# An attention and feed-forward kernel: three layout changes moved to DMA transfers, a feed-forward from exact bf16 parts, and one of fourteen additions done by an accumulating transfer

## The chip, the cores and the metric

One core of a Trainium2 chip runs the whole program. The metric is the device time of one execution in microseconds (us). The kernel before took 4421.93 us as the median of three runs (4421.24 to 4422.01).

## What is computed

The input `x` is 4 sequences of 2048 rows of 512 float32 values. Queries, keys and values are projections with three 512x512 matrices, for 16 heads of 32 columns. Attention is added to `x` and each row is normalised. A feed-forward with the signs of a 512x512 matrix follows, and it is scaled and shifted by column and clipped; it is added to the normalised rows, and each row is normalised again:

```python
q = (x @ Wq.T).reshape(N, S, H, hd).transpose(0, 2, 1, 3)   # k, v the same way; H = 16, hd = 32
energy = jnp.einsum('nhqd,nhkd->nhqk', q, k)
attn = jax.nn.softmax(energy / jnp.sqrt(jnp.float32(hd)), axis=3)
out = jnp.einsum('nhql,nhld->nhqd', attn, v)
...
x = _layernorm(x + out)
w = (weights >= 0.0) * 2.0 - 1.0
y = jnp.clip(jnp.einsum('bsi,oi->bso', x, w) * scale + bias, -100.0, 100.0)
x = _layernorm(x + y)
```

Everything is float32, and the kernel keeps float32 products.

## The kernel before

The work is cut into 16 groups `n`: one sequence `b` and four heads (`g`) each. A group has four blocks `qb` of 512 queries, and a block has 16 steps, one for each chunk `kc` of 128 keys. So there are 64 blocks and 1024 steps. The engines are named PE (matrix products), DVE (vector), ACT (activations and copies), POOL (GpSimd) and SP (which issues transfers).

In each step PE does this, in this order:

- `scores` (L306, L312): for four heads, minus the row maximum (three bf16 parts against ones) plus keys times queries. ACT takes the exponentials into a tile `p` of 128x2048 float32 (L319). There are four such tiles in turn (`ppool`).
- `max_unit` (L247): scores of a later block, 22 steps ahead (`LEAD`), for the row maxima. DVE reduces three of the four heads out of PSUM (L254), and ACT copies the fourth to a tile `moved`, which DVE reduces at the end of the step.
- fillers: projections (L206), transposes, feed-forward, sums. A planner gives each a first and a last step and hands out at most two large ones in odd steps.
- `weighted` (L330): every second step, two chunks of probabilities times values into one PSUM bank, which DVE adds to `oT` (L342).

After these, `add_up` lets POOL add the chunk's `p` to `acc` (L350): 14 additions of 128x2048 a block, of which the first takes two chunks. Then come the actions that `at(step, ...)` put at the end of a step: loads, statistics, normalisation, stores. Each engine runs its own instructions in the order in which the program emits them, and PSUM has eight banks, which `take` and `give` hand out by a running estimate of when each comes free.

Three things at the edge of a block matter here. Five steps ahead of a block `max_parts` (L279 to L283) makes the final row maxima and cuts them into three bf16 parts, and `max_rows` turns them with four PE transposes (L290), which ACT copies to `negm` (L295). Some three steps after a block, `denominators` sums the exponentials over keys: PE multiplies the last `p` and `acc` by ones (L356), ACT copies the result to `dT` (L382), and `reciprocals` turns it back with four PE transposes (L390) for DVE (L397). `add_attention` turns `oT` (L390), multiplies by the reciprocals (L414), adds columns of `x` (L418) and stores to a DRAM tensor `res`.

When all four groups of a sequence are done, `Finish` takes blocks of 512 rows, as four tiles of 128 rows: `stats` (L463, L464), `norm` (L489), `turn` (four PE transposes L499, one ACT copy L502 to `nT`), `ffn` in three thirds of 172, 172 and 168 columns (four float32 products each, L510; then DVE adds the bias from PSUM, clips in PSUM and adds to the row, L515, L516, L518), and `stats` and `norm` again. This runs beside the attention of the next sequence, so the first quarter of the time has none of it. The last two of the 16 blocks of rows are finished at the end of the program, in whole width. The signed and scaled weights are made once by POOL (L148, L150) from the raw matrix.

On DVE, every operation with two tensors reads at least one of them from PSUM.

Of the kernel before, what the change touches and what calls it, by code (L numbers as in the profile page):

```python
# [20 lines left out]
def kernel(  # L21
# [35 lines left out]
    stage = ctx.enter_context(tc.tile_pool(name="stage", bufs=4))  # L57
# [9 lines left out]
    work = ctx.enter_context(tc.tile_pool(name="work", bufs=2))  # L67
# [37 lines left out]
    ident_bf = const.tile([P, P], BF16, name="ident_bf")  # L105
    nc.vector.tensor_copy(ident_bf, ident)
# [38 lines left out]
    def sign_weights():  # L145

        ws = raws["ws"]
        nc.gpsimd.tensor_scalar(ws, ws, 0.0, 2.0, ALU.is_ge, ALU.mult)  # L148
        for oc in range(DC):
            nc.gpsimd.tensor_scalar(  # L150
                ws[:, oc, :], ws[:, oc, :], 1.0, scale_t[:, oc : oc + 1], ALU.subtract, ALU.mult
            )

    raws = {n: load_weight(w, n) for n, w in (("wk", wk), ("wq", wq))}
    scale_t = const.tile([P, DC], F32, name="scale_t")
    bias_bc = const.tile([P, D], F32, name="bias_bc")

    def load_rest():
        for n, w in (("wv", wv), ("ws", w_ffn)):
            raws[n] = load_weight(w, n)  # L160
        nc.sync.dma_start(out=scale_t, in_=ffn_scale.rearrange("(c p) -> p c", p=P))
        nc.sync.dma_start(out=bias_bc, in_=ffn_bias.partition_broadcast(P))
# [15 lines left out]
    rec = {}  # L178

# [95 lines left out]
    def max_parts(n, qb, i):  # L275
# [7 lines left out]
        nc.vector.tensor_tensor(sp[:, :, :, 2], nm, sp[:, :, :, 1], ALU.subtract)  # L283

    def max_rows(n, qb):
        sp = split[qb % 2]
        i = take()
        pt = ps[:, i, : QB // 2].bitcast(BF16)
        for qc in range(NTQ):
            nc.tensor.transpose(  # L290
                pt[:, ts(qc, P)], sp[:, qc, :, :].rearrange("p h d -> p (h d)"), ident_bf
            )
        negm[n, qb] = small.tile([P, QB], BF16, tag="negm", name="negm")
        runs("full", 0.23)
        nc.scalar.copy(negm[n, qb], pt)  # L295
        give(i, "ACT", 0.6)
# [48 lines left out]
    def add_up(n, qb, kc, p, before):  # L345
        if kc == 1:
            acc[n, qb] = apool.tile([P, HG, QB], F32, tag="acc", name="acc")
        if 0 < kc < (NT // 2 if is_last(n, qb) else NT - 1):
            a = acc[n, qb]
            nc.gpsimd.tensor_tensor(a, before if kc == 1 else a, p, ALU.add)  # L350
        if kc == NT - 1:
            last_p[n, qb] = p
# [20 lines left out]
    def denominators(n, qb):  # L373
# [3 lines left out]
        else:  # L377
            b = take()
            ones_times(b, last_p.pop((n, qb)), True, False)
            ones_times(b, acc.pop((n, qb)), False, True)  # L380
        dT = once.tile([P, QB], F32, tag="dT", name="dT")
        nc.scalar.copy(dT, ps[:, b, :])  # L382
        give(b, "ACT", 0.6)
        acc[n, qb] = dT

# [7 lines left out]

    def reciprocals(n, qb):
        i, pd = turn_back(acc.pop((n, qb)))
        rec[n, qb] = small.tile([P, NTQ, HG, 1], F32, tag="rec", name="rec")
        nc.vector.reciprocal(rec[n, qb], pd[:, :, :, 0:1])  # L397
        give(i, "DVE", 0.3)
# [30 lines left out]
    class Finish:  # L429
        def __init__(self, b, g):  # L430
            self.b, self.g = b, g
            self.mv, self.rs, self.nb, self.nT, self.rows_rs = {}, {}, {}, {}, {}

# [60 lines left out]

        def turn(self, j):
            i = take()
# [4 lines left out]
            self.nT[j] = work.tile([P, DC, P], F32, tag="nT", name="nT", bufs=4)  # L501
# [3 lines left out]
        def ffn(self, j, third):  # L505
            cols = slice(0, D) if third is None else slice(THIRDS[third], THIRDS[third + 1])
            i = take()
            py = ps[:, i, : cols.stop - cols.start]
            for c in range(DC):
                nc.tensor.matmul(  # L510
                    py, lhsT=self.nT[j][:, c, :], rhs=wT["ws"][:, c, cols],
                    start=(c == 0), stop=(c == DC - 1),
                )
            runs("full", 6.8e-3 * (cols.stop - cols.start))
            nc.vector.tensor_tensor(py, py, bias_bc[:, cols], ALU.add)  # L515
            nc.vector.tensor_scalar(py, py, MAX_VAL, -MAX_VAL, ALU.min, ALU.max)  # L516
            dst = self.row(j)[:, cols]
            nc.vector.tensor_tensor(dst, dst, py, ALU.add)  # L518
            give(i, "DVE", 0.5 + 3.1e-3 * (cols.stop - cols.start))
# [30 lines left out]
    def finish(b, qb, a, every, w, lag):  # L550
        f = Finish(b, qb)
        at(a, f.load)
        for j in range(NTQ):
            at(a + 2 + j, f.stats, 1, j)
        at(a + 6, f.rstd, 1)
        at(a + 7 + lag, f.shift, 1)
        for j in range(NTQ):
            t = a + 8 + lag + every * j
            at(t, f.norm, 1, j)
            turned = task("small", t + 1, t + 3, f.turn, j)  # L560
            for k in range(3):
                task("big", t + 2, t + w, f.ffn, j, k, after=turned)
            at(t + w, f.stats, 2, j)
        e = a + 9 + lag + every * (NTQ - 1) + w
        at(e, f.rstd, 2)
        at(e + 1 + lag, f.shift, 2)
        for j in range(NTQ):
            at(e + 2 + lag + j, f.norm, 2, j)
        at(e + 5 + lag, f.store)

    def finish_last(qb, last):
# [4 lines left out]
        late = qb == NQB - 2  # L576
        for j in range(NTQ):
# [3 lines left out]
        ffns = []  # L581
        for j in range(NTQ):
            t = a + 5 + (j if late else 2 * j)
            by = t + 6
            at(t, f.norm, 1, j)
            if late:
                by = total + (-1, 1, 4, 5)[j]
            turned = task("small", t + 1, t + 3, f.turn, j, after=ffns[j - 2] if j > 1 else None)
            for k in [None] if late else range(3):
                ffn = task("big", by if late else t + 2, by, f.ffn, j, k, after=turned)  # L590
            ffns.append(ffn)
# [222 lines left out]
```

## Time and profile before

| | before |
|---|---|
| median of three runs | 4421.93 us |
| the profiled execution | 4420.69 us |
| its span in the profile | 4418.7 us |
| granted clock of PE | 0.999 |
| busy PE | 4380.8 us (99%) |
| busy POOL | 4083.3 us (92%) |
| busy DVE | 3320.2 us (75%) |
| busy ACT | 3048.4 us (69%) |

The span runs from the first to the last instruction of one execution. The busy time of an engine is the time in which at least one of its instructions is under way; for PE the ends of matrix products are modelled, so that starts are the safer thing to compare. A row of the groups view has line, engine, operation, output and inputs with their shapes, how many there are, then the busy time, the mean duration of one in ns, and the idle time before them with what ended it. A float32 product shows as two records.

### The profile page before, as it was taken

The page shows a single profiled execution, that of the slowest core. Times are in us where ns is not written, and L with a number is a line of the kernel's source. Part 1 is how long each engine was busy: PE and PEld are TensorE (multiplying, and loading weights), DVE is VectorE, ACT ScalarE, POOL GpSimd, SP SyncE. Part 2 cuts the span into 40 slices and gives each one's busy share as a digit, 9 for nine tenths or more (in the row PEclk, how much of TensorE's full clock was granted, in tenths as well). Part 3 has the DMA queues.
Part 4 walks back from the last instruction along what each step waited for, and adds up shares of the span by engine and source line. Part 5 has one row for each costly group of instructions (what it writes and reads, how often), then busy time and mean ns, then how long its engine had stood idle before and what let it go on. Part 6 is the DMA issues. An engine that isn't in the chain of part 4 may idle for free.

```text
span 4418.7 us, 94451 instructions
## 1 busy us (share of the span) xinstructions
PE 4380.8 (99%) x38648; PEld 2261.4 (51%) x38648; DVE 3320.2 (75%) x5909; ACT 3048.4 (69%) x6493; POOL 4083.3 (92%) x940
## 2 busy tenths in 40 slices
PE   9999999999999999999999999999999999999998
PEld 5554444454555555555555555555555555555443
DVE  6777777777777777777777777777777777777774
ACT  5666666676667667677676766767667676767675
POOL 3999999999999999999999999999999999999994
PEclk9999999999999999999999999999999999999999
DMA  3000000010000000011000000001000000000001
GB/s 91 6 11 11 6 11 11 9 39 28 6 11 30 6 20 20 6 42 32 20 20 6 30 11 16 20 7 48 16 20 20 18 18 20 16 20 30 13 23 45
DMA packets 98019, 92.30 MB, mean 21 GB/s; under 512 B 4272, under 2 KB 73904, under 8 KB 97584
## 3 DMA queue, kind: packets, MB, share of 16 engines
q1 hardware_dynamic: 92304, 82.07, 6.2%
q8 instruction: 302, 4.95, 0.5%
q10 hardware_dynamic: 5280, 4.19, 0.3%
q14 instruction: 133, 1.09, 0.1%
HBM read 53.74 MB, written 32.51 MB: 20 GB/s over the span
## 4 chain that ended last, share of the span: by engine, by line
PE 89%; POOL 8%; ACT 1%; issue 1%; DVE 1%; DMA 0%; ACTq 0%; POOLq 0%; DVEq 0%
PE ps L330 19%; PE ps L247 18%; PE ps L312 18%; PE ps L206 15%; POOL acc L350 8%; PE ps L306 7%; PE ps L510 5%; PE ps L356 3%; PE ps L390 2%; PE ps L499 1%; PE ps L195 1%; ACT p L319 1%; DVE part L254 1%; PE ps L290 0%; ACT xg_last L489 0%
## 5 line engine op out<-in xcount | busy, mean ns | idle before, releaser
L350 POOL TENSOR_TENSOR acc<-acc,p 128x2048 f32<-128x2048 f32 x825 | 3743.2, 4537 | 106.1 <-ACT p L319 49.3
L319 ACT ACTIVATE p<-ps 128x512 f32<-128x512 f32 x4096 | 2115.0, 604 | 1148.4 <-PE ps L312 1113.8
L254 DVE TENSOR_REDUCE part<-ps 128x1 f32<-128x512 f32 x3072 | 1934.8, 684 | 821.1 <-PE ps L247 820.2
L247 PE MATMUL ps<-kT,qT 32*128 32x512 f32 x8192 | 1098.1, 590 | 0.0
L312 PE MATMUL ps<-qT,kT 32*128 32x512 f32 x8192 | 1070.7, 590 | 0.0
L330 PE MATMUL ps<-p,vv 128*32 128x512 f32 x8192 | 983.6, 598 | 0.5 <-ACT p L319 0.3
L247 PEld LDWEIGHTS ps<-kT,qT 32*128 32x128 f32 x8192 | 524.0, 185 | 379.8 <-issue 221.0
L254 DVE TENSOR_REDUCE part<-moved 128x1 f32<-128x512 f32 x1024 | 691.2, 675 | 1.7 <-ACT moved L266 1.6
L266 ACT COPY moved<-ps 128x512 f32<-128x512 f32 x1024 | 634.5, 620 | 21.8 <-PE ps L247 16.7
L330 PEld LDWEIGHTS ps<-p,vv 128*32 128x32 f32 x8192 | 220.3, 109 | 685.6 <-issue 346.5
L306 PE MATMUL ps<-negm,ones_bf 32*128 32x512 bf16 x4096 | 434.9, 384 | 3.9 <-ACT p L319 1.3
L312 PEld LDWEIGHTS ps<-qT,kT 32*128 32x128 f32 x8192 | 405.6, 184 | 38.3 <-issue 20.4
L350 POOL TENSOR_TENSOR acc<-p 128x2048 f32<-128x2048 f32 x64 | 290.8, 4544 | 132.4 <-ACT p L319 132.3
L342 DVE TENSOR_TENSOR oT<-ps,oT 128x512 f32<-128x512 f32 x448 | 309.8, 692 | 90.1 <-PE ps L330 57.6
L306 PEld LDWEIGHTS <-ones_bf 32*128 32x128 bf16 x4096 | 104.3, 91 | 496.9 <-issue 438.3
L206 PEld LDWEIGHTS ps<-wvT,xT 128*128 128x128 f32 x2048 | 244.6, 191 | 67.7 <-ACT p L319 62.1
L206 PE MATMUL ps<-wvT,xT 128*128 128x128 f32 x2048 | 270.3, 280 | 1.4 <-ACT p L319 0.5
L206 PEld LDWEIGHTS ps<-xT,wkT 128*128 128x128 f32 x2048 | 242.4, 191 | 48.2 <-ACT p L319 46.7
L206 PE MATMUL ps<-xT,wkT 128*128 128x128 f32 x2048 | 265.1, 279 | 0.5 <-ACT p L319 0.2
L206 PE MATMUL ps<-xT,wqT 128*128 128x128 f32 x2048 | 262.2, 277 | 1.1 <-ACT p L319 1.0
L510 PE MATMUL ps<-wsT,nT 128*128 128x172 f32 (+2 forms) x1408 | 259.3, 329 | 2.4 <-ACT nT L502 1.1
L206 PEld LDWEIGHTS ps<-xT,wqT 128*128 128x128 f32 x2048 | 245.2, 192 | 25.5 <-ACT p L319 23.0
(74 smaller groups left out, 1831.2 us busy)
## 6 DMA issues: line engine op xcount, KB each, us to landing
xs<-in_L_attn_x_dram SPq DMA_DIRECT2D x64, 256.0 KB, 2.8
xc<-in_L_attn_x_dram SPq DMA_DIRECT2D x60, 256.0 KB, 3.2
res<-xc SPq DMA_DIRECT2D x60, 256.0 KB, 2.4
xg<-res SPq DMA_DIRECT2D x12, 1024.0 KB, 6.1
out_dram<-xg SPq DMA_DIRECT2D x12, 1024.0 KB, 4.8
xg_last<-res SPq DMA_DIRECT2D x4, 768.0 KB, 6.1
out_dram<-xg_last SPq DMA_DIRECT2D x3, 1024.0 KB, 4.3
raw_wk<-in_L_attn_Wk_dram ACTq DMA_DIRECT2D x4, 256.0 KB, 6.3
```

The costliest lines, as they stand in the source:

```text
L206: nc.tensor.matmul(pp, lhsT=lhs(c), rhs=rhs(c), start=(c == 0), stop=(c == DC - 1))
L247: nc.tensor.matmul(ps[:, banks[h], :], lhsT=qT[n, qb][rows, ts(qc, P)], rhs=kT[n][rows, ts(kb, QB)], start=True, stop=True,)
L254: nc.vector.tensor_reduce(part[:, qc, h : h + 1, kb], src, AX.X, ALU.max, negate=True)
L266: nc.scalar.copy(moved, ps[:, banks[-1], :])
L306: nc.tensor.matmul(ps[:, banks[h], :], lhsT=ones_bf[rows, :], rhs=negm[n, qb][rows, :], start=True, stop=False,)
L312: nc.tensor.matmul(ps[:, banks[h], :], lhsT=kT[n][rows, ts(kc, P)], rhs=qT[n, qb][rows, :], start=False, stop=True,)
L319: nc.scalar.activation(p[:, h, :], ps[:, banks[h], :], AF.Exp, scale=SM_SCALE)
L330: nc.tensor.matmul(pb[cols, :], lhsT=vv[n][:, kc, cols], rhs=p[:, h, :], start=(i == 0), stop=(i == 1),)
L342: nc.vector.tensor_tensor(outs[n, qb], pb, outs[n, qb], ALU.add)
L350: nc.gpsimd.tensor_tensor(a, before if kc == 1 else a, p, ALU.add)
L356: nc.tensor.matmul(ps[h * HD : (h + 1) * HD, b, :], lhsT=ones, rhs=p[:, h, :], start=start, stop=stop,)
L510: nc.tensor.matmul(py, lhsT=self.nT[j][:, c, :], rhs=wT["ws"][:, c, cols], start=(c == 0), stop=(c == DC - 1),)
```

## The change

- `max_rows` is gone: `max_parts` ends with a transposing DMA transfer, issued by SP, from the 128x512 bf16 parts to `negm`.
- `turn` and the float32 `ffn` are replaced for 14 of the 16 blocks of rows (56 tiles). ACT copies the normalised row to bf16 (`part_high`), DVE subtracts that (`less_high`), ACT copies the rest to bf16 (`part_middle`), DVE subtracts again (`part_low`), one action a step; a transposing transfer turns the 128x1536 bf16 parts to `nT`. `ffn` is then twelve bf16 products a third, with weights of plus and minus one. ACT copies each third to a tile `y` in SBUF. DVE multiplies by the scale (`scaled`), adds the bias and clips (`clipped`), and adds to the row (`added`). Tiles follow each other by 12 steps (10 in the third sequence) instead of 13 and 11.
- For 63 of 64 blocks the sums go by DMA: ACT copies them, SP stores four rows of 512 to DRAM, and SP loads them as 128x16 single values; DVE's reciprocal is put two steps after.
- The addition of the chunk `kc` = 14 is a transfer on POOL's queue that adds `p` to `acc` in SBUF.
- The signs and the scaled weights are made by twelve DVE operations, one every two steps, from step 80 on.
- `stage` has three buffers instead of four, and `work` one instead of two.

```diff
+        negm[n, qb] = small.tile([P, QB], BF16, tag="negm", name="negm")
+        nc.sync.dma_start_transpose(
+            out=negm[n, qb].rearrange("p (t q) -> p t q", t=NTQ),
+            in_=sp.rearrange("p t h d -> p (t h d)"),
+        )
...
-        if 0 < kc < (NT // 2 if is_last(n, qb) else NT - 1):
+        if 0 < kc < (NT // 2 if is_last(n, qb) else NT - 2):
             a = acc[n, qb]
             nc.gpsimd.tensor_tensor(a, before if kc == 1 else a, p, ALU.add)
+        elif kc == NT - 2 and not is_last(n, qb):
+            nc.gpsimd.dma_start(out=acc[n, qb], in_=p, accum_op=ALU.add)
...
+    def columns_of_sums(n, qb):
+
+        dT = acc.pop((n, qb))
+        rows = dram.tile([HG, QB], F32, tag="sums", name="sums", bufs=2)
+        nc.sync.dma_start(out=rows, in_=dT.rearrange("(h r) q -> h r q", h=HG)[:, 0, :])
+        sums_of[n, qb] = small.tile([P, HG * NTQ], F32, tag="sums", name="sums")
+        with nc.allow_non_contiguous_dma(reason="2048 single sums"):
+            nc.sync.dma_start(
+                out=sums_of[n, qb], in_=rows.rearrange("h (t p) -> p (h t)", p=P)
+            )
...
+        def part_high(self, j):
+            self.parts[j] = work.tile([P, 3, D], BF16, tag="parts", name="parts")
+            nc.scalar.copy(self.parts[j][:, 0, :], self.row(j))
...
+        def less_high(self, j):
+            self.left[j] = work.tile([P, D], F32, tag="left", name="left")
+            nc.vector.tensor_tensor(
+                self.left[j], self.row(j), self.parts[j][:, 0, :], ALU.subtract
+            )
...
+        def part_middle(self, j):
+            nc.scalar.copy(self.parts[j][:, 1, :], self.left[j])
...
+        def part_low(self, j):
+            parts = self.parts.pop(j)
+            nc.vector.tensor_tensor(
+                parts[:, 2, :], self.left.pop(j), parts[:, 1, :], ALU.subtract
+            )
...
+            nc.sync.dma_start_transpose(
+                out=self.nT[j], in_=parts.rearrange("p k d -> p (k d)")
+            )
...
+        def ffn(self, j, third):
+
+            cols = slice(THIRDS[third], THIRDS[third + 1])
+            i, py = self.times_weights(j, ws_bf, cols, 0.86)
...
+            nc.scalar.copy(self.y[j][:, cols], py)
+            give(i, "ACT", 0.3)
+
+        def scaled(self, j):
+            nc.vector.tensor_tensor(self.y[j], self.y[j], scale_bc, ALU.mult)
+
+        def clipped(self, j):
+            nc.vector.tensor_tensor(self.y[j], self.y[j], bias_bc, ALU.add)
+            nc.vector.tensor_scalar(self.y[j], self.y[j], MAX_VAL, -MAX_VAL, ALU.min, ALU.max)
+
+        def added(self, j):
+            nc.vector.tensor_tensor(self.row(j), self.row(j), self.y.pop(j), ALU.add)
...
+    def parted(f, t, j):
+
+        at(t, f.norm, 1, j)
+        at(t + 2, f.part_high, j)
+        at(t + 3, f.less_high, j)
+        at(t + 4, f.part_middle, j)
+        at(t + 5, f.part_low, j)
...
+            t = a + 13 + every * j
+            parted(f, t, j)
+            by = t + every - 1
             for k in range(3):
-                task("big", t + 2, t + w, f.ffn, j, k, after=turned)
+                task("big", t + 7, by, f.ffn, j, k)
+            at(by, f.scaled, j)
+            at(by + 2, f.clipped, j)
+            at(by + 3, f.added, j)
+            at(by + 4, f.stats, 2, j)
```

## The prediction

> **What bounds the kernel now.** I read the page's busy row first, then its chain, then POOL's timeline block by block, then one step's timeline. The busy row and the groups:
>
> ```profile
> PE 4380.8 (99%) x38648; PEld 2261.4 (51%) x38648; DVE 3320.2 (75%) x5909; ACT 3048.4 (69%) x6493; POOL 4083.3 (92%) x940
> PE ps L330 19%; PE ps L247 18%; PE ps L312 18%; PE ps L206 15%; POOL acc L350 8%; PE ps L306 7%; PE ps L510 5%; PE ps L356 3%; PE ps L390 2%; PE ps L499 1%; PE ps L195 1%; ACT p L319 1%; DVE part L254 1%; PE ps L290 0%; ACT xg_last L489 0%
> ...
> L350 POOL TENSOR_TENSOR acc<-acc,p 128x2048 f32<-128x2048 f32 x825 | 3743.2, 4537 | 106.1 <-ACT p L319 49.3
> L342 DVE TENSOR_TENSOR oT<-ps,oT 128x512 f32<-128x512 f32 x448 | 309.8, 692 | 90.1 <-PE ps L330 57.6
> ```
>
> PE is full, but 8% of the chain is POOL's additions. POOL's timeline tells where:
>
> ```profile
> 418.26 4.57 POOL L350 TENSOR_TENSOR acc<-p 128x2048 f32<-128x2048 f32 x1
> 422.90 59.90 POOL L350 TENSOR_TENSOR acc<-acc,p 128x2048 f32<-128x2048 f32 x13
> 482.76 4.56 POOL L350 TENSOR_TENSOR acc<-p 128x2048 f32<-128x2048 f32 x1
> ...
> 1463.68 4.54 POOL L350 TENSOR_TENSOR acc<-p 128x2048 f32<-128x2048 f32 x1 [0.64 <-ACT p L319]
> ...
> 1478.35 50.69 POOL L350 TENSOR_TENSOR acc<-acc,p 128x2048 f32<-128x2048 f32 x11 [0.21 <-ACT p L319]
> 1531.21 4.54 POOL L350 TENSOR_TENSOR acc<-p 128x2048 f32<-128x2048 f32 x1 [2.17 <-ACT p L319]
> ```
>
> From 418 to 934 us and once more at 1065 a block takes 64.5 us with no gap: 14 additions at 4.607 us from start to start. POOL bounds these nine blocks. Later, where the feed-forward runs beside attention, a block takes 67.5 us and POOL sits idle for some 4 us of it: PE bounds, but POOL is inside an addition 94% of the time (63.5 of 67.5).
>
> **What goes from PE.** I count from start to start, since ends are modelled.
> - Turning maxima: L290's four transposes start 56 ns apart, and the next float32 product starts 0.256 us after the fourth: 0.42 us x 64 = 27 us.
> - Turning sums: 63 x 4 transposes at 0.109 us = 27 us. Turning rows: 56 x 4 x 0.109 = 24 us.
> - Feed-forward: a float32 third is eight passes 0.146 us apart, 1.17 us. A bf16 third is twelve passes. Their pitch is not in the trace; L290 gives 56 ns for 128 columns, so 75 ns for 172, and L306 (four of 512 columns in 0.216 us) gives 72. That is 0.89 us a third. Where a float32 product follows, the 0.2 us of L290's exit is added; in the new order that is so for some 37 thirds. 168 x 0.28 - 37 x 0.2 = 40 us.
>
> Sum: 118 us, where PE bounds. In the nine POOL-bound blocks the dropped addition counts instead: 64.5 falls to 13 x 4.607 = 59.9 us plus the issue of the transfer, or to what PE needs there (about 60); I take 61.5, so 27 us in place of the 8 us of PE. Net gain about 135 us. ACT loses two copies and gains five per tile; at 69% that stays hidden.
>
> **What comes in on DVE.** Out go 3 x (0.335 + 0.345 + 0.332) = 3.0 us a tile (L515, L516, L518). In come six operations of 512 columns: five at L342's 0.69 us and the clip (0.35 to 0.7), about 4 us. By load alone nothing happens: DVE is at 77% in this stage (207.7 of 269.3 us in the window from 1397.2).
>
> But all six have only SBUF operands, which no DVE operation with two tensors has now. One row of before is near, a DVE cast from SBUF to SBUF at the program's start:
>
> ```profile
> 1.24 0.98 POOL L119 MEMSET split<- 128x512 bf16 x2
> 1.32 0.98 DVE L106 CAST ident_bf<-ident 128x128 bf16<-128x128 f32 x1 [1.32 <-POOL ident masks.py:199]
> ```
>
> 128 elements took 0.98 us, more than the 0.69 us of 512 elements in L342, and the cast ended 0.08 us after POOL's two memsets. The Trainium skill (SBUF — State Buffer, section "Who interferes with whom") states the rule that fits and that speaks against this change: DVE's second pair of SBUF ports is GpSimd's only pair, a DVE operation with two SBUF inputs, or in a two-port mode, contends with a GpSimd operation that reads SBUF, and the later one "fully blocks" until the other ends. The trace shows this beside memsets only, not beside additions. By the rule, such an operation waits out the 4.54 us addition that is under way; by load, it costs 0.69 us and is hidden. I take the rule, since L106 is the only row of its kind.
>
> How much delay can DVE take? Here is a step, with `stats` where the change puts its operations (after the reduction of `moved`):
>
> ```profile
> 1411.47 9.17 POOL L350 TENSOR_TENSOR acc<-acc,p 128x2048 f32<-128x2048 f32 x2
> 1412.49 0.68 DVE L254 TENSOR_REDUCE part<-moved 128x1 f32<-128x512 f32 x1
> 1412.76 1.03 PE L247 MATMUL ps<-kT,qT 32*128 32x512 f32 x8
> 1413.08 0.68 DVE L463 BATCH_NORM_STATS2 st<-xg 128x6 f32<-128x512 f32 x1
> 1413.90 1.85 DVE L254 TENSOR_REDUCE part<-ps 128x1 f32<-128x512 f32 x3
> 1416.09 0.39 PE L306 MATMUL ps<-negm,ones_bf 32*128 32x512 bf16 x4
> ```
>
> A blocked operation here would wait from 1413.1 to 1416.0, run to 1416.7, and only then would the three maxima free their banks. I did this for each of the 744 steps from 1130 to 4350 us. The wait is what is left of POOL's instruction when `moved` is done: 2.18 us on average. The room is the least, over the next DVE instructions, of the time between one's end and PE's next write of its bank, plus DVE's idle time until then: median 1.5 us, a tenth under 0.8, a tenth over 2.6. Wait plus 0.69 us less room, where positive, averages 1.45 us. That is PE standing still, and what queues behind on DVE are the maxima and `oT`, which PE needs.
>
> Per tile there are five steps with such an operation, so 56 x 5 x 1.45 = 406 us. As blocks get longer, POOL is inside an addition less (60 us of 73, not 94%): times 0.85, 345 us. The clip follows the bias addition, and POOL's next addition may come in between: 0 to 4.5 us each; I take a third, 56 x 1.5 x 0.85 = 70 us. POOL's own delay, 6 x 0.7 us a tile, is covered by the addition it lost; without that it would bound the block (64.5 + 4.2 > 67.5).
>
> **Transfers.**
> - nT: issued at the end of step t+5, wanted by PE's fillers in t+7, about 4.7 us after DVE's place in t+5. 384 KB lies between `xs` (256 KB, 2.8 us) and `xg` (1024 KB, 6.1 us), so 3.4 us for a plain transfer; for transposes no row exists, so 3 to 8 us. At 3.4 nothing, at 8 about 4 us x 52 tiles. I take 20 us. Ahead of it on SP stand only transfers whose producers are emitted earlier.
> - negm: 128 KB, five steps (about 19 us) ahead, hidden unless it takes that long.
> - Sums: a store (2.0 us is the nearest, `out_dram<-xg_last`) and a load of 2048 single values (`scale_t`, 512 values, 2.5 us; I take 4), some 7 us with issue. The reciprocal stands two steps later, about 9.5 us after ACT's copy. Hidden, with 2 us to spare; DVE waits if it is later, 63 x the excess, at most 100 us.
> - The accumulating transfer: 1 MB, 4.8 us for a plain store to perhaps 12. It starts after POOL's 13th addition; PE wants the sum, and ACT the `p` tile, four steps after its chunk. Room about 10 us. I take nothing; 63 x 2 us if it takes 12. Its issue on POOL (1 to 3 us) has the lost 4.6 us as cover.
>
> Sum: 345 + 70 + 20 - 135 = +300 us on the profiled 4420.7, which is 1.2 us under the median: 4725.
>
> **Rivals.**
> - DVE does not wait for a whole addition (ports shared, or only memset and cast collide). For it: the DVE rows here all run beside additions at a steady 0.69 us; but they read PSUM. Then 0.69 us goes into room of 1.5 us, and what stays is -135 + 20 to 50 us: 4305, 4285 to 4385. It decides at a wait of 0.8 us; below that the change is faster.
> - A part of the wait (half an addition at most, or five operations where POOL is between blocks): 4390 to 4560.
> - A transfer is late: if the transposes took 15 us, PE would wait 11 us x 52 tiles, +570 us, alone enough for 4860; against it, the landing times above. That transposing transfers work element by element is the form in which the change would not do what it says.
>
> **Numbers.** The full wait 0.64 (4560 to 4940), a part of it 0.13, no wait 0.20, late transfers 0.03. Predicted 4725. The range 4340 to 4900 leaves out the better part of the no-wait case and the top of the full wait. Faster by over 0.2% (9 us, about what a measurement of this kernel can tell from no change): 0.22; within 0.2%: 0.02; slower: 0.76.
>
> **What would show it.** Right: the five new DVE rows with a mean near 2.9 us instead of 0.69, a row of PE waiting for DVE's maxima, POOL's busy share near 80%, blocks of some 73 us in the last three sequences and of about 61.5 us at 420 to 930 us. Wrong: means below 1.2 us in these rows, or a long wait of PE for `nT`, `negm` or `acc`, or of DVE for `sums`.

## The result, and the profile after

The changed kernel takes 4994.95 us (median of four runs, 4990.74 to 5003.59), against 4421.59 us for the kernel before on the same chip: a ratio of 1.1299 (95% interval 1.1280 to 1.1319). It is slower by 573 us where I forecast 300 (4725 us), and lies above the range, which ended at 4900.

The page of the changed kernel, its busy row, the granted clock in 40 slices, the chain by line, and the groups that answer to those shown of before:

```profile
PE 4542.3 (91%) x38588; PEld 2278.8 (46%) x38588; DVE 4019.0 (81%) x5752; ACT 3098.0 (62%) x6653; POOL 3878.8 (78%) x935
...
PEclk9999999999999999999999999999999999999988
...
PE ps L248 12%; PE ps L306 11%; PE ps L324 11%; POOL acc L345 11%; DVE part L255 9%; PE ps L207 7%; PE ps L300 5%; DMA nT<-parts 4%; PE ps L565 3%; DVE parts L535 3%; DVE y L589 3%; DMA acc<-p 2%; PE ps L353 2%; DVE y L585 2%; ACT p L313 2%
...
L345 POOL TENSOR_TENSOR acc<-acc,p 128x2048 f32<-128x2048 f32 x762 | 3496.6, 4589 | 363.8 <-ACT p L313 315.1
```

PE has fewer instructions than before (38,588 for 38,648), yet 161 us more busy time, and is down to 91% of the span. The chain now holds DVE (L255, L535, L589, L585) and two transfers, `nT` and `acc`. POOL, the co-bound of before, is at 78% and idles behind ACT. A busy time that rises while work falls is the first hint of a slower clock: the `PEclk` row shows only whole tenths, so I took windows (the third number from the end of a row is the granted clock):

```profile
90.00:418.00 328.00, 322.29 (x2893) 161.66 (x2892) 236.38 (x397) 221.44 (x476) 298.87 (x70) 1.00 0.12 24
...
1100.00:2000.00 900.00, 820.00 (x6997) 411.20 (x6995) 748.52 (x1051) 554.85 (x1194) 719.60 (x170) 0.95 0.17 35
...
4400.00:4980.00 580.00, 482.48 (x3776) 227.77 (x3768) 455.77 (x601) 334.79 (x727) 378.12 (x100) 0.91 0.18 40
```

Before, every such window shows 1.00. After, it is 0.99 to 1.00 where there is no feed-forward and 0.91 to 0.96 where there is. The clock records of the trace have 70 falls to half speed, 413 us in all (one more, at the very end, stands in the trace of before too), worth up to some 206 us of PE's work.

The six new DVE operations, by form:

```profile
L535 DVE TENSOR_TENSOR parts<-left,parts 128x512 bf16<-128x512 f32 x56 | 201.7, 3603 | 2.5 <-ACT parts L530 2.5
L590 DVE TENSOR_SCALAR y<-y 128x512 f32<-128x512 f32 x48 | 163.0, 3397 | 1.6
L589 DVE TENSOR_TENSOR y<-y,bias_bc 128x512 f32<-128x512 f32 x48 | 162.1, 3378 | 0.0
L585 DVE TENSOR_TENSOR y<-y,scale_bc 128x512 f32<-128x512 f32 x48 | 146.9, 3061 | 0.0
L524 DVE TENSOR_TENSOR left<-xg,parts 128x512 f32<-128x512 f32 x48 | 94.1, 1960 | 0.0
...
L594 DVE TENSOR_TENSOR xg<-xg,y 128x512 f32<-128x512 f32 x48 | 46.8, 975 | 0.0
```

Where L336, with an operand in PSUM, still takes 687 ns, the same number of columns out of SBUF takes up to 3.6 us: these instructions wait for POOL. Here is one tile's bias addition (L589) and clip (L590), and what they do to PE (timeline):

```profile
2252.22 4.54 POOL L345 TENSOR_TENSOR acc<-p 128x2048 f32<-128x2048 f32 x1 [9.35 <-ACT p L313]
...
2253.26 4.05 DVE L589 TENSOR_TENSOR y<-y,bias_bc 128x512 f32<-128x512 f32 x1
...
2253.42 1.02 PE L306 MATMUL ps<-qT,kT 32*128 32x512 f32 x8
...
2256.84 4.85 POOL L345 TENSOR_TENSOR acc<-acc,p 128x2048 f32<-128x2048 f32 x1
...
2257.34 4.64 DVE L590 TENSOR_SCALAR y<-y 128x512 f32<-128x512 f32 x1
...
2261.90 1.87 DVE L255 TENSOR_REDUCE part<-ps 128x1 f32<-128x512 f32 x3
2262.64 1.18 PE L300 MATMUL ps<-negm,ones_bf 32*128 32x512 bf16 x3 [3.45 <-DVE part L255]
...
2263.24 2.28 PE L306 MATMUL ps<-qT,kT 32*128 32x512 f32 x8
```

The bias addition starts 1 us after POOL's addition and ends 0.55 us after it. The clip, though it has one input, is caught by POOL's next addition and ends 0.29 us after that one. The clip waits for a whole addition or not at all: of the 56 clips 21 take 0.43 us, 35 take 4.6 us, and none lies between. In the view of line L590 (least, median and greatest duration in ns):

```profile
L590 DVE TENSOR_SCALAR y<-y x48: 426/4616/4639, 1264.4 to 4639.8; 128x512 f32<-128x512 f32 x48
```

For 8.6 us DVE reads no maxima out of PSUM; PE has to wait for a bank and stands for 3.45 us. Then eight L306 products take 2.28 us, where the eight at 2253.42 took 1.02. The granted clock in three windows around this place:

```profile
2256.00:2261.20 5.20, 3.19 (x29) 0.74 (x22) 5.17 (x2) 2.12 (x5) 5.12 (x2) 1.00 0.10 7
2261.20:2268.00 6.80, 5.37 (x23) 2.75 (x23) 5.32 (x9) 2.54 (x5) 0.94 (x2) 0.50 0.11 1
2268.00:2275.00 7.00, 7.00 (x69) 3.71 (x70) 6.96 (x11) 4.17 (x9) 5.57 (x2) 1.00 0.14 37
```

This pause is paid twice: 3.45 us of standing, and 6.8 us at half speed, which begin 2 us into it. Over the whole trace, PE's gaps above 0.15 us grow from 17 us in 36 gaps to 426 us in 224. Of the 62 gaps of 2.5 us or more, 60 are followed by half speed; of the 100 below 1 us, 4. In between it goes either way.

The start times of the falls show what decides there. They all lie on one grid of 3.413 us, and what counts is how long PE stood in the 3.413 us just before. That was 1.7 us or more before 67 of the 70 falls, and in only 4 of the 1336 stretches of the grid at full speed that no fall follows (in d8, below: before 37 of 37, and in 2 of 1303). So 1.7 us of standing within one stretch is enough here, and a pause of 2.5 us that is spread over two stretches can pass.

What PE and ACT wait for (total us, times, longest us):

```profile
PE ps L300 <- DVE part L255: 236.3, 111, 6.0
...
PE ps L565 <- DMA nT<-parts: 65.5, 42, 6.2
...
ACT p L313 <- DMA acc<-p: 49.2, 16, 5.1
...
PE ps L353 <- ACT p L313: 35.2, 18, 4.0
```

The last two belong to the accumulating transfer, also where there is no feed-forward. POOL's timeline, then the step after the transfer's issue, in the sequence that was to gain:

```profile
693.16 0.88 POOL L347 DMA_DIRECT2D acc<-p  x1 [0.30 <-POOL acc L345]
695.89 4.50 POOL L345 TENSOR_TENSOR acc<-p 128x2048 f32<-128x2048 f32 x1 [1.85 <-ACT p L313]
702.40 4.53 POOL L345 TENSOR_TENSOR acc<-acc,p 128x2048 f32<-128x2048 f32 x1 [2.02 <-ACT p L313]
709.60 50.73 POOL L345 TENSOR_TENSOR acc<-acc,p 128x2048 f32<-128x2048 f32 x11 [2.67 <-ACT p L313]
760.63 0.88 POOL L347 DMA_DIRECT2D acc<-p  x1 [0.30 <-POOL acc L345]
763.34 4.50 POOL L345 TENSOR_TENSOR acc<-p 128x2048 f32<-128x2048 f32 x1 [1.83 <-ACT p L313]
```

```profile
700.19 2.06 ACT L313 ACTIVATE p<-ps 128x512 f32<-128x512 f32 x4 [3.40 <-DMA acc<-p]
...
700.84 1.50 PE L353 MATMUL ps<-p,ones 128*32 128x512 f32 x8 [2.31 <-ACT p L313]
```

POOL is late in these blocks, so the transfer is issued at 693.16, only after the last addition, and holds its `p` tile for 7 us. ACT waits for that tile, PE for ACT, and POOL for ACT. A block takes 67.5 us (695.89 to 763.34) instead of 64.5.

### The profile page after: what moved, and what is told of

Same layout as the page of the kernel before. It is cut to its first block, busy times and chain, and to the rows that moved or that the text cites. A ratio compares the mean times of both kernels' runs of the same rounds, so it can differ in the third digit from the quotient of the medians.

```text
span 4988.9 us, 94806 instructions
## 1 busy us (share of the span) xinstructions
PE 4542.3 (91%) x38588; PEld 2278.8 (46%) x38588; DVE 4019.0 (81%) x5752; ACT 3098.0 (62%) x6653; POOL 3878.8 (78%) x935
## 4 chain that ended last, share of the span: by engine, by line
PE 52%; DVE 23%; POOL 11%; DMA 7%; issue 5%; ACT 2%; ACTq 0%; POOLq 0%; SPq 0%; DVEq 0%
PE ps L248 12%; PE ps L306 11%; PE ps L324 11%; POOL acc L345 11%; DVE part L255 9%; PE ps L207 7%; PE ps L300 5%; DMA nT<-parts 4%; PE ps L565 3%; DVE parts L535 3%; DVE y L589 3%; DMA acc<-p 2%; PE ps L353 2%; DVE y L585 2%; ACT p L313 2%
## 5 line engine op out<-in xcount | busy, mean ns | idle before, releaser
L345 POOL TENSOR_TENSOR acc<-acc,p 128x2048 f32<-128x2048 f32 x762 | 3496.6, 4589 | 363.8 <-ACT p L313 315.1
L255 DVE TENSOR_REDUCE part<-ps 128x1 f32<-128x512 f32 x3072 | 1931.7, 682 | 707.7 <-PE ps L248 706.3
L248 PE MATMUL ps<-kT,qT 32*128 32x512 f32 x8192 | 1235.3, 614 | 24.1 <-DVE part L255 14.3
L306 PE MATMUL ps<-qT,kT 32*128 32x512 f32 x8192 | 1150.0, 617 | 0.0
L248 PEld LDWEIGHTS ps<-kT,qT 32*128 32x128 f32 x8192 | 588.0, 191 | 457.4 <-issue 222.0
L300 PE MATMUL ps<-negm,ones_bf 32*128 32x512 bf16 x4096 | 503.8, 391 | 266.6 <-DVE part L255 236.3
L255 DVE TENSOR_REDUCE part<-moved 128x1 f32<-128x512 f32 x1024 | 690.9, 675 | 4.8 <-ACT moved L267 4.7
L300 PEld LDWEIGHTS <-ones_bf 32*128 32x128 bf16 x4096 | 116.6, 91 | 776.2 <-issue 716.1
L306 PEld LDWEIGHTS ps<-qT,kT 32*128 32x128 f32 x8192 | 422.7, 190 | 70.8 <-issue 54.1
L336 DVE TENSOR_TENSOR oT<-ps,oT 128x512 f32<-128x512 f32 x448 | 307.6, 687 | 86.7 <-PE ps L324 60.1
L207 PE MATMUL ps<-xT,wqT 128*128 128x128 f32 x2048 | 273.7, 284 | 0.0
L565 PE MATMUL ps<-ws_bf,nT 128*128 128x172 bf16 (+1 forms) x1728 | 154.6, 247 | 65.5 <-DMA nT<-parts 65.5
```

Of the source, the lines that this page charges most:

```text
L207: nc.tensor.matmul(pp, lhsT=lhs(c), rhs=rhs(c), start=(c == 0), stop=(c == DC - 1))
L248: nc.tensor.matmul(ps[:, banks[h], :], lhsT=qT[n, qb][rows, ts(qc, P)], rhs=kT[n][rows, ts(kb, QB)], start=True, stop=True,)
L255: nc.vector.tensor_reduce(part[:, qc, h : h + 1, kb], src, AX.X, ALU.max, negate=True)
L300: nc.tensor.matmul(ps[:, banks[h], :], lhsT=ones_bf[rows, :], rhs=negm[n, qb][rows, :], start=True, stop=False,)
L306: nc.tensor.matmul(ps[:, banks[h], :], lhsT=kT[n][rows, ts(kc, P)], rhs=qT[n, qb][rows, :], start=False, stop=True,)
L336: nc.vector.tensor_tensor(outs[n, qb], pb, outs[n, qb], ALU.add)
```

## The experiments

My theory after this result: the six DVE operations wait for POOL, as forecast, and the forecast lacked the clock that PE loses after each longer pause; the accumulating transfer costs where it was taken as free. Rivals: the transposing transfers, or the sum of DVE's load rather than its long absences.

### The parts one by one

Each is the kernel before with one part of the change. p1_negm turns the row maxima by transfer:

```diff
-            task("small", first - 3, first - 3, max_rows, n, qb)
+        nc.sync.dma_start_transpose(
+            out=negm[n, qb].rearrange("p (t q) -> p t q", t=NTQ), in_=...)
```

> The kernel before with one part of the change: the maxima are turned by the transposing transfer, not by four PE transposes. If transfers that come late are what made the change slow: slower than 4422 us, with PE waiting for negm. If they are hidden, and the time is PE's: 64 x 0.42 us less on PE, of which nine blocks bound by POOL keep theirs (-4 us), so about 4399 us, no clock loss.

Measured: 4396.19 us, ratio 0.9944 (0.9929 to 0.9959). A gain of 25 us; the transfer is hidden.

p2_sums turns the sums by a store and a load (`columns_of_sums`) in place of four PE transposes.

> The kernel before with one part of the change: the sums go through DRAM by two transfers and the reciprocal stands two steps later. If late transfers made the change slow: DVE waits for the load of 2048 single values, and the time is over 4422 us by some us a block (60 to 200 us in all). If hidden: 63 x 4 x 0.109 = 27 us less PE, about 4399 us.

Measured: 4400.94 us, ratio 0.9953 (0.9937 to 0.9970). A gain of 21 us.

p3_acc adds chunk 14 by the accumulating transfer:

```diff
-        if 0 < kc < (NT // 2 if is_last(n, qb) else NT - 1):
+        if 0 < kc < (NT // 2 if is_last(n, qb) else NT - 2):
...
+        elif kc == NT - 2 and not is_last(n, qb):
+            nc.gpsimd.dma_start(out=acc[n, qb], in_=p, accum_op=ALU.add)
```

> The kernel before with one part of the change: the addition of chunk 14 by the accumulating transfer. First reckoning of the prediction: nine blocks fall from 64.5 to 61.5 us, so 4395 us. Reckoning from the trace after: POOL is behind in those blocks, the transfer (7.4 us to landing) starts late and holds its p tile, ACT waits for it up to 5 us, PE stands still for over 2.5 us and runs at half clock for 3.4 us after it; 5 + 1.7 us against 3 us gained in each of some nine blocks, so 4440 to 4470 us, granted clock about 0.995.

Measured: 4467.41 us, ratio 1.0106 (1.0090 to 1.0121): 46 us slower, with 34 us at half clock. POOL is relieved (86% for 92%), but ACT waits for the transfer, in its waits:

```profile
ACT p L319 <- DMA acc<-p: 61.5, 24, 4.8
```

p4_ffn has the bf16 feed-forward with its transposing transfers and nothing else.

> The change without its other three parts: only the feed-forward from bf16 parts, with its DVE operations from SBUF and the twelve operations for the weights (POOL adds all fourteen chunks, maxima and sums are turned by PE). If the DVE operations that wait for POOL's additions are the cause: most of the 573 us is here, 4880 to 5050 us, the rows of the five DVE operations at 2 to 3.6 us, granted clock 0.95 to 0.97. If the transfers of the other three parts are the cause: under 4500 us.

Measured: 4947.74 us, ratio 1.1192 (1.1175 to 1.1208), clock 0.964. So 526 of the 573 us come with this part.

### Within the changed kernel: without the waits, without the transfer, without both

a_nolock replaces the six DVE operations by reductions with one input of the same size. It leaves out what they compute (the differences of the split, scale, bias, clip and residual).

```diff
-            nc.vector.tensor_tensor(self.y[j], self.y[j], scale_bc, ALU.mult)
+            one_in(self.y[j], self.y[j])     # tensor_reduce; the other five alike
```

> The kernel after, where each of the six DVE operations of a tile (both subtractions, scale, bias, clip, addition) is replaced by a copy of the same 512 columns as a reduction over an axis of one: one SBUF input, about 0.68 us, so this part of the arithmetic is left out. If waiting for POOL's additions is the cause: these rows fall to 0.7 us, PE's idle time from 426 to under 120 us, the granted clock rises to 0.99 and the time is 4340 to 4430 us. If the load on DVE, the transfers or the new order of work are the cause: over 4800 us.

Measured: 4455.5 us, ratio 1.0077 (1.0062 to 1.0092). The stand-ins take 0.66 to 0.68 us beside the same additions; half clock falls from 413 to 51 us. The waits with their clock are thus worth 540 us. But the time stays above that of before, and above what I expected. Its waits name the transfer:

```profile
ACT p L316 <- DMA acc<-p: 113.5, 45, 6.6
...
PE ps L356 <- ACT p L316: 70.9, 47, 5.5
```

a_noacc is the changed kernel with POOL doing the addition of chunk 14 again.

> The changed kernel with POOL adding the block's last chunk again (4.54 us on POOL per block) in place of the accumulating transfer. Theory: alone the transfer cost 46 us, and PE's waits that begin with it (49 us of ACT behind the transfer, 35 us of PE behind ACT) go, while the DVE waits and the clock they cost (about 540 us) stay: 4930 to 4970 us. Rival: POOL, already held up by the same shared waits as DVE, gets 63 x 4.54 = 286 us more to do and is the bound of the blocks: the time is as with the transfer or above it, 4990 to 5060 us.

Measured: 4922.39 us, ratio 1.1131 (1.1113 to 1.1150): 73 us better, a little more than my theory had. One more wait went with the transfer: PE's wait for `nT`, 65.5 us in the changed kernel, is

```profile
PE ps L563 <- DMA nT<-parts: 16.1, 36, 2.0
```

here. So the accumulating transfer also delays the transposed rows. The timeline of the changed kernel shows how:

```profile
2152.91 4.79 DVE L535 TENSOR_TENSOR parts<-left,parts 128x512 bf16<-128x512 f32 x1
2157.45 0.88 POOL L347 DMA_DIRECT2D acc<-p  x1 [0.30 <-POOL acc L345]
2157.77 5.53 SPq L543 DMA_TRANSPOSE nT<-parts  x1
2168.09 1.90 PE L565 MATMUL ps<-ws_bf,nT 128*128 128x172 bf16 x12 [6.23 <-DMA nT<-parts]
```

The last subtraction (L535) waits for the same addition on POOL as the accumulating transfer, so both transfers are issued together. Nine transposes are issued within 1.5 us after an accumulating transfer. Their issue takes 4.0 to 5.5 us instead of 1.45 (the median), and pauses of PE of 3.9 to 6.2 us follow, 50 of the 65.5 us. In a_nolock, which has the transfer but not the waits, PE's matrix products wait 3.1 us for `nT` in all: this cost needs both parts of the change.

a_nolock_noacc is both edits together, with the same work left out as in a_nolock.

> As a_nolock (the six feed-forward instructions with two inputs on DVE replaced by reductions of one input, so the layer norm's scale and shift, the bias, the residual and the two differences of the split are left out), and POOL adds the last chunk in place of the accumulating transfer. Theory: what kept a_nolock 34 us above before was the transfer that starts late (113 us of ACT waiting for it, 71 us of PE behind that) and its share of the clock; without it the feed-forward in bf16 and the turned parts show their saving on PE (feed-forward rows 48, turned rows 28, sums 31, maxima 28 us): 4421 - 135 = 4286 us if POOL keeps up, up to 4350 where POOL's adds bound the blocks. Rival: it is not the transfer, but DVE having too much to do beside the maxima (PE's L251 rows at 139 ns against 126 before), and the time stays at 4430 us or more.

Measured: 4378.93 us, ratio 0.9902 (0.9887 to 0.9917): the transfer costs 77 us here too, so the rival falls. The saving that remains is 44 us, though, not 70 to 135. The page and POOL's timeline say why:

```profile
PE 4290.8 (98%) x38588; PEld 2156.8 (49%) x38588; DVE 3395.0 (78%) x5752; ACT 3080.9 (70%) x6653; POOL 4071.3 (93%) x935
```

```profile
1407.57 4.54 POOL L348 TENSOR_TENSOR acc<-p 128x2048 f32<-128x2048 f32 x1 [1.44 <-ACT p L316]
...
1473.05 4.55 POOL L348 TENSOR_TENSOR acc<-p 128x2048 f32<-128x2048 f32 x1 [0.50 <-ACT p L316]
...
1538.10 4.54 POOL L348 TENSOR_TENSOR acc<-p 128x2048 f32<-128x2048 f32 x1
```

These two blocks beside the feed-forward take 65.3 us each; over 44 such blocks it is 66.1 us on average, where before it was 67.8. POOL's fourteen additions need 64.5: PE got less work than POOL lets it use.

A second reason stands in the first sequence. The twelve operations for the weights are kept in this run, and they work out of SBUF beside POOL's additions too. Four of them as they ran in the changed kernel (2.8 us each), then the starts of the two blocks of a_nolock_noacc in which eleven of the twelve fall:

```profile
L151 DVE TENSOR_TENSOR wsT<-ws_bf,scale_bc 128x512 f32<-128x512 bf16 x4 | 11.3, 2828 | 0.0
```

```profile
414.68 4.73 POOL L348 TENSOR_TENSOR acc<-p 128x2048 f32<-128x2048 f32 x1
...
493.55 4.55 POOL L348 TENSOR_TENSOR acc<-p 128x2048 f32<-128x2048 f32 x1 [8.53 <-ACT p L316]
...
563.29 4.55 POOL L348 TENSOR_TENSOR acc<-p 128x2048 f32<-128x2048 f32 x1 [2.34 <-ACT p L316]
```

They take 78.9 and 69.7 us, where the blocks around them take 64.9: some 19 us. No run moves these operations alone.

### Does a long absence of DVE take the clock?

d5 and d8 are the kernel before with idle reductions on DVE (0.684 us each, one input, no wait for POOL), one after the other at one place in each of 44 blocks (the profile has 220 and 352 of them; the expectations count 47 blocks, which the edit does not give):

```diff
+    def held_up(k):
+        for _ in range(k):
+            nc.vector.tensor_reduce(junk, bias_bc, AX.X, ALU.max)
...
+            if b and n < N - 1:
+                at(first + 7, held_up, 5)      # d8: 8
```

> The kernel before, with five idle reductions of 512 columns (3.4 us of DVE) put at the end of one step of each block of the last three sequences (47 blocks), where DVE has 1.5 us of room in the median. Each should hold PE up by some 1.9 us. By the room alone: 47 x 1.9 = 90 us, 4510 us. If a pause of PE costs its clock only from about 2.5 us on, as the trace after has it, the granted clock stays near 0.998 here.

> The same with eight reductions (5.4 us): PE is held up by some 3.9 us each time. By the room alone, with no loss of clock: 47 x 3.9 = 185 us, 4607 us, so 95 us more than with five. With half clock for at least 3.4 us after each pause over 2.5 us (1.7 us lost or more): 47 x 5.6 = 263 us, 4685 us or more, so 175 us more than with five, at a granted clock of about 0.98.

Measured, with two runs each: d5 4512.5 us, ratio 1.0206 (1.0186 to 1.0227); d8 4671.09 us, ratio 1.0565 (1.0544 to 1.0586). Three more reductions, 2.05 us of DVE in 44 blocks or 90 us, cost 159 us. In d8 the longest waits of PE are well past the point where the clock falls, in d5 they only touch it (3 falls, against 37 in d8); first d5, then d8:

```profile
PE ps L312 <- DVE part L260: 35.3, 33, 2.0
```

```profile
PE ps L312 <- DVE part L260: 131.2, 46, 4.1
```

Half clock is 14 us in d5 and 212 us in d8. The clock is lost without any of the change's operations, by a longer hold-up alone. d5 shows one more thing: of its 92 us only 35 lie in PE's gaps and 7 in the clock. PE's busy time at full clock grew by the other 50, with the same instructions, so a part of PE's waiting is counted as busy.

d8_spread has d8's eight reductions, but one in each of eight steps:

```diff
-                at(first + 7, held_up, 8)
+                for k in range(8):
+                    at(first + 7 + k, held_up, 1)
```

> As d8: 8 idle reductions of 0.684 us on DVE in each of 47 blocks, but one in each of eight steps instead of eight in a row. Theory: what costs is how long DVE is away from the maxima at a stretch (a room of about 1.5 us, and from a pause of about 2.5 us on the half clock as well), so 0.68 us at a time costs next to nothing and the clock stays at 0.999: 4421 to 4435 us. Rival: DVE's total matters, the room is not refilled between the steps: 5.5 us less 1.5 in each of 47 blocks, about 4600 us, or 4671 with the loss of clock that d8 had.

Measured: 4422.53 us against 4421.9 for before, ratio 1.0004 (0.9995 to 1.0013). The same number of reductions, 237 us of extra DVE work, cost nothing; this window of its trace has DVE at 84% and PE full at full clock:

```profile
1200.00:2200.00 1000.00, 998.73 (x8912) 521.23 (x8904) 835.05 (x1493) 694.73 (x1475) 944.35 (x214) 1.00 0.07 21
```

a_split is the changed kernel with the bias addition and the clip one step apart; no work is left out and none added:

```diff
+        def biased(self, j):
             nc.vector.tensor_tensor(self.y[j], self.y[j], bias_bc, ALU.add)
+            spend("DVE", 0.6)
...
             at(by, f.scaled, j)
+            at(by + 1, f.biased, j)
             at(by + 2, f.clipped, j)
```

> The changed kernel with one edit: the bias add and the clip of a tile (3.4 us each, one right after the other) are issued in two successive steps instead of one. The same instructions, the same waits for the port. Theory: the pair makes one pause of about 6.8 - 1.5 = 5.3 us, the longest of a tile, which is always followed by the half clock; apart they make two of 1.9 us, below the 2.5 us from which the clock falls. Gain: a second room of 1.5 us in 56 tiles (84 us) and more than half of the 206 us of lost clock: 4750 to 4830 us at a granted clock of 0.98. Rival: the lead that PE has over DVE is not refilled within one step, so that the two pauses are as one, or single instructions make pauses above 2.5 us as well: 4930 to 4995 us at 0.96.

Measured: 4769.25 us (4754.14 to 4770.27), ratio 1.0778 (1.0762 to 1.0794), clock 0.982: 226 us come back. PE's gaps fall from 426 to 264 us and half clock from 413 to 164 us. One thing in my expectation was off: the waits for POOL are not the same. In the rows by form the addition and the clip now take

```profile
L593 DVE TENSOR_SCALAR y<-y 128x512 f32<-128x512 f32 x48 | 111.5, 2322 | 0.0
...
L589 DVE TENSOR_TENSOR y<-y,bias_bc 128x512 f32<-128x512 f32 x48 | 74.4, 1551 | 0.0
```

3.9 us together instead of 6.8, while the residual addition L597 rises from 1.0 to 1.8: how long one waits depends on where POOL's additions lie. So a part of the gain (about 2.5 us a tile over the six rows, some 120 us of DVE time) is shorter waiting, and PE's wait for `nT` falls too, from 65.5 to 32.3 us. How the 226 us divide between these, the second room and the clock, I can't separate; the counts of gaps and of lost clock overlap, since part of a pause can lie in the half-clock time.

### Versions meant to be faster

c1 tried to keep the bf16 feed-forward without the waits: the subtractions on POOL, scale, bias, clip and residual on DVE in PSUM, the weights' signs on POOL, the last sequence in float32, and the accumulating transfer from the second sequence on.

> The parts of the change without a DVE operation that reads two tensors from SBUF: maxima and sums by transfers; the feed-forward of the first three sequences from bf16 parts, with both subtractions on POOL, scale, bias, clip and addition on DVE from PSUM by thirds, and the transpose two steps after the last subtraction; the weights' signs on POOL as before; the accumulating transfer from the second sequence on only, where POOL is not behind; the last sequence's feed-forward in float32 as before. If the waits of DVE and the pauses of PE are all that spoilt the change: 4422 - 23 - 21 - 48 x 0.8 = about 4340 us, clock 0.999. If bf16 parts or late transfers cost by themselves: over 4380 us, with PE waiting for nT.

Measured: 4476.2 us, ratio 1.0123 (1.0106 to 1.0140). The waits for the port are gone and PE is 98% busy, but `ACT p L321` waits 65.5 us for the transfer, and POOL, with two subtractions of 1.2 us a tile more, starts a block every 68 to 71 us (1399.44, 1467.46, 1538.48 in its timeline). Neither reckoning came true: the time is over 4380 us, but PE does not wait for `nT` to speak of. Whether POOL's subtractions or the transfer decide, I did not separate.

p12 is the kernel before with the two parts that gained, negm and sums.

> The kernel before with two parts of the change alone: the row maxima turned by a transposing transfer (p1_negm) and the sums turned by two transfers (p2_sums); the feed-forward and the adds on POOL are those of before. My theory: the two gains are of different matmuls and copies (a block's turned maxima, a block's turned sums) and add up: 4421.6 - 25 - 21 = about 4375 us, 4368 to 4384. Rival: both gains come from the same slack of PE at the block's boundary, so that together they give little more than one: about 4395 us.

Measured: 4376.95 us (4376.0 to 4377.2), ratio 0.9895 (0.9880 to 0.9910). The gains add up to 45 us. POOL is at 93% now, so that further savings on PE would come up against its additions (inferred from its share, not tested):

```profile
PE 4338.9 (99%) x38140; PEld 2234.1 (51%) x38140; DVE 3318.2 (76%) x5909; ACT 3018.0 (69%) x6429; POOL 4083.9 (93%) x940
```

Of the versions that compute everything this is the fastest, and it beats both kernels.

## Why the prediction was wrong in size and right in direction

The direction was right; the size failed in three terms of my sum: the clock after long pauses, which I left out, the accumulating transfer, which I took as free, and the gain, which I took too large. The runs split the 573 us along these terms. Each entry is a difference of medians (the forecast sum gives 4722 us; I rounded it to 4725):

| term | forecast | measured | from |
|---|---|---|---|
| waits of DVE for POOL (345 + 70) | +415 | +540 | after less a_nolock |
| accumulating transfer | 0 | +77 | a_nolock less a_nolock_noacc |
| gain and `nT` (-135 + 20) | -115 | -44 | a_nolock_noacc less before |
| sum | +300 | +573 | |

**The waits themselves: right in the mechanism, in the sum partly by luck.** Five operations at 2.18 us of waiting each, and the clip's 1.5, make 12.4 us a tile. The rows show 3.60 + 3.40 + 3.38 + 3.06 + 1.96 + 0.98 = 16.4 us for operations that need some 0.68 us each, the clip 0.43, so 12.5 us of waiting. But the single means differ (0.3 to 2.9), and the clip meets POOL's next addition in 35 of 56 tiles, not in a third of them; the errors cancel. The Trainium skill's rule on the shared port pair (SBUF — State Buffer, "Who interferes with whom") held beside additions on POOL too, where before had shown it beside two memsets only. a_nolock shows the other side of it: a reduction with one input out of SBUF takes 0.68 us. The clip shows that one input is no protection by itself; by that section an operation in a two-port mode contends as well, and `tensor_scalar` can enter one. No trace records the mode, but where it does not wait the clip takes 0.43 us out of SBUF, and 0.70 with the same columns in PSUM (L601).

**The standing still: about right.** 345 + 70 us were forecast for it. PE's gaps are 426 us, and 124 us in a_nolock, which keeps everything but the waits: 302 us. Another 100 us lie in PE's busy time at full clock, which is that much longer than in a_nolock for the same instructions. If this is waiting counted as busy, as d5 suggests, the standing comes to some 400 us; no run shows it apart.

**The missing term: the clock.** The step that failed is "Wait plus 0.69 us less room, where positive, averages 1.45 us. That is PE standing still". I took a mean and priced the standing alone. What follows a pause depends on its length: below 1 us next to nothing, from 2.5 us on nearly always half speed, mostly for 3.4 or 6.8 us. Half-clock time is 362 us longer than in a_nolock. Without what lies inside the pauses it is 332 us against 57, so some 137 us of PE's work; the waits were under-priced by 125 us. d8 against d5, and d8_spread against d8, show this without the change. The Trainium skill has the rule (TensorE: Matmul & The Clock Gate, "Why this matters for your kernels": no idle gaps of PE above some 3 us between bursts); here less is enough, 1.7 us of standing within 3.4. I weighed the port's rule and did not ask what the pauses it makes would do to the clock. By the mean of 1.45 us no pause would have cost it. But the mean hides the spread: with the wait of each of the 744 steps and the median room of 1.5 us, 23% of the single pauses come out above 2.5 us (an estimate from the trace of before). And the pair of bias addition and clip, one after the other, made a pause of 2.5 us or more in 40 of the 56 tiles.

**"I take nothing" for the accumulating transfer: wrong.** It lands in 7.4 us, inside the 4.8 to 12 that I gave. The error was the room, "about 10 us": in blocks where POOL is behind, the transfer's issue stands behind POOL's thirteenth addition and starts late, so it holds `p` just where ACT needs it. In p3_acc it cost 46 us, in the other two pairs 73 and 77, in the pair with the waits mostly through `nT` (49 us less of PE's wait for it without the transfer). The blocks of the first sequence were to fall from 64.5 to 61.5 us; the one shown rose to 67.5.

**The gain: too large.** On PE the bf16 products came out as forecast (72 to 75 ns from start to start; I had taken 72 to 75), and the 0.2 us on return to float32 that I feared did not appear. But I capped only the nine blocks of the first sequence by POOL's 64.5 us. With PE's work reduced, a_nolock_noacc runs into the same bound in the blocks beside the feed-forward (66.1 us on average). And the sum has no term for the twelve operations for the weights, which wait for POOL as well (some 19 us). That these two make up the missing 71 us is read from the timeline, not tested.

**The transposing transfers: right by themselves.** `negm` is hidden (p1_negm), the sums as well (p2_sums), and `nT` without the other transfer's company costs PE 16 us; I had 20. With it PE waits 65.5 us, which I did not foresee.

The signs: POOL's busy share (78%, forecast 80), PE's wait for the maxima (236 us) and the long DVE rows came as said. One sign against it came too, the long wait of PE for `nT` (65.5 us). The last three sequences took 79.6 us a block ((4988.9 - 1166.4) / 48), not 73; this counts the end of the program too. The clock and the transfer come on top.

## What to carry to other kernels

Price a stall by its length, not its mean: here pauses of PE below 1 us cost little more than themselves, those from 2.5 us on nearly always a half-speed stretch as well. So spread long operations of a feeding engine over steps (d8_spread: 237 us of extra DVE work for nothing; a_split: 226 us back for moving one instruction, a part of them by shorter waits). Before moving DVE's operands from PSUM to SBUF, see what POOL does at that time. Two operations that wait for the same third one will also end together, and so may the transfers that follow them (`nT` and `acc`). And when two engines share the bound, a saving on one is worth only the way to the other: ask for each block, not for the average.

## What of the hardware I had not expected

- A `TENSOR_SCALAR` on DVE with a single SBUF input (the clip) waits beside POOL's additions like those with two inputs (3.40 us mean; 0.43 where it does not wait), while a reduction (0.68 us) and `BATCH_NORM_STATS2` (0.68 us), also out of SBUF, do not.
- POOL's own 128x512 subtraction took 1.2 us in c1, less than the same on DVE beside POOL (2.0 to 3.6 us).
- The accumulating transfer's issue costs POOL 0.88 us, and the landing takes 7.4 us for 1 MB. A transposing transfer issued within 1.5 us after it takes 4.0 to 5.5 us to issue on SP, 1.45 us otherwise (median).
- Falls of the clock start on a grid of 3.413 us, after 1.7 us or more of standing in the stretch before (67 of 70).
